# A fused four-layer image kernel: side stages begun earlier, one transfer for each part of a sum, and inverse deviations by logarithm and exponential

## The chip, the cores and the metric

The kernel runs on 1 core of one Trainium2 chip. The metric is the device time of one execution in microseconds. Before the change the median of three runs is 13,699.78 us (13,695.32 to 13,710.06). All engines of the core work: TensorE (PE) multiplies matrices, VectorE (DVE), ScalarE (ACT) and GpSimd (POOL) work on tiles of up to 128 partitions, and SyncE (SP) issues almost all transfers between the chip's memory (HBM) and the core's SBUF.

## What is computed

Four images of 96 channels and 64 x 64 points go through four layers, each `x = x + layer(group_norm(x))`. Layer 0 is an attention over a pooled image with a neighbourhood softmax, layer 2 a 3 x 3 convolution. Layers 1 and 3 each hold a four-way selective scan over the 4096 points: the image read by rows and by columns, forwards and backwards, with 192 channels of 16 states. Cut to the scan of layer 3 (layer 1 has the same recurrence in another form):

```
def step(h, inp):
    d, uu, bb, cc = inp
    h = h * jnp.exp(d[..., None] * A) + (d * uu)[..., None] * bb[:, :, None, :]
    y = jnp.einsum('bkdn,bkn->bkd', h, cc)
    return (h, y)
...
y = oy[:, 0] + inv[:, 0] + why + invwhy          # the sum of the four directions
y = layernorm_last(jnp.transpose(y, (0, 2, 1)).reshape(B, H, W, Di), ong, onb)
return y * jax.nn.silu(z) @ ow.T
```

Layer norms over channels follow the sum of the four directions in both layers, and another one stands in layer 3. They need 1 / sqrt(variance + 1e-5) for each point. Group norms (32 groups of 3 channels over all points) stand ahead of each layer.

## The kernel before, in words

**Units.** Layer and image give eight scans, in the order of `SCANS`: layer 1 of images 0 and 1, layer 3 of images 0 and 1, layer 1 of images 2 and 3, layer 3 of images 2 and 3. Here they are numbered 0 to 7. A scan has four directions, each cut into 4 chunks of 1024 points and 2 halves of 96 channels: 32 groups. A group is cut into 12 units of 8 channels times 16 states (128 partitions x 1024 points). So a scan has 384 units, and the kernel 3072. In the text "unit 361" is counted within a scan.

**A unit** (`unit`, L2167) issues, in an order written out by hand, the load of `rep` four units ahead (`fetch`, L2068), its decays two units ahead on ACT (L2076), its own scan on DVE (`scan`, L2096), the product with C on POOL (`times_c`, L2108), the product of the next unit's input with B on DVE (`times_b`, L2089), and the matmul that makes that input two units ahead (`drive`). Every four units `collect` sums states on PE into `acc`, and after a group's last collect `output` copies `acc` to `yo`, which a transfer stores into `y_row` or `y_col` at the start of the next unit. The list `stored` counts the groups that are stored. Each engine runs its instructions in the order in which they are issued; SP's queue holds all loads and stores.

**`prepare(g)`** makes a group's decays' exponents and inputs two groups ahead. For the first half of each chunk it needs the chunk's two halves of u (`load_u`, L1962). They are loaded ahead only within a scan; for the first chunk of the next scan `prepare` loads them itself, in unit 366 of the scan before, and its matmul stands one unit later.

**Stages.** Everything else is a generator that is resumed up to three times a unit through `Slots.begin`: a `yield` tells how many slots of 0.5 us of budget a step is put down at, a bare `yield` stands after matmuls, which are put down at their own estimate. `PACE[s]` is the budget of a unit of scan s. `beside(s)` says which stages run beside scan s: `first` (layer 0 and the input side of layer 1), `second` (the output side of layer 1, layer 2, the input side of layer 3), `third` (the output side of layer 3) and `last` (the same for the last image, in blocks). Scans 0, 3 and 4 have a `first` beside them; 1, 2, 5 and 6 a `second`, that of the image whose layer-1 scan has just ended; 7 has three `third` and the `last`. A stage begins at unit 0; at unit 365 `work.run()` issues all that is left of it at once. In the steps of the program, `second` stages are done at units 353 to 360 and leave nothing to `work.run()`; scans 0, 3 and 4 leave it 8, 24 and 8 steps.

**Sums of the four directions** (`directions`, L1529). Each half image has 4 parts (chunks) of 96 channels x 1024 points, stored as four blocks of 24 rows with gaps of 8. `ungapped` (L1118) loads a part with four transfers of 24 rows, 96 KB each. `directions` waits until the scan's last groups are stored, loads all parts of one half (32 transfers), goes on, and does the same for the other half. Then 16 steps add the two images on PE and copy them back on ACT.

**`layer_norm`** (L1261) collects the variances of 8 (or 2) pieces in one PSUM tile, makes `lines`, the inverse deviations of 8 x 512 (or 2 x 512) points, by a square root on ACT (L1292) and a reciprocal on DVE (L1294), and broadcasts each line to 96 partitions by a matmul. It is called 18 times beside or behind the scans. **`group_norm_on_scalar`** (L1161) does its passes over the image on ACT; 14 calls.

Of the kernel before, what the change touches and what calls it, by code (L numbers as in the profile page):

```python
# [9 lines left out]
F32 = mybir.dt.float32  # L10
# [17 lines left out]
CH = 1024  # L28
NCH = L // CH
# [9 lines left out]
          (("first", 3),), (("second", 2),), (("second", 3),), (("third", 0), ("third", 1), ("third", 2), ("last", 3)))  # L39
GN_EPS = 1e-5  # L40
PHI_EPS = 1e-12
PACE = (2.95,3.45,3.45,2.95,2.95,3.45,3.45,3.2)


PHI_SAFE = 10.0
# [855 lines left out]
def streams(ctx: ExitStack, tc: tile.TileContext, x, wts, cst, out, wat, cat, flag):  # L901
# [215 lines left out]

    def ungapped(dst, src, cols):  # L1118

        for q in range(4):  # L1120
            nc.sync.dma_start(out=dst[24 * q : 24 * q + 24], in_=src[32 * q : 32 * q + 24, cols])

    def group_norm(src, dst):

# [32 lines left out]
    def group_norm_on_scalar(src, dst):  # L1161

        st = small.tile([96, 8], F32, name="gs_st")
        for j in range(4):
            s = src[:, bass.ts(j, CH)]
            nc.scalar.activation(s, s, AF.Copy, accum_out=st[:, j : j + 1])
            yield 1
        mv = small.tile([96, 4], F32, name="gs_mv")
        nc.vector.tensor_reduce(mv[:, 0:1], st[:, 0:4], AX.X, ALU.add)
        yield 0.5  # L1170
        p = bank()
        mm(p[:96, 0:1], group[:96], mv[:, 0:1])
        yield
        nc.scalar.activation(mv[:, 1:2], p[:96, 0:1], AF.Copy, scale=-1.0 / L)
        yield 0.5
        for j in range(8):
            p = bank()
            nc.scalar.activation(p[:96], src[:, bass.ts(j, PCH)], AF.Square, bias=mv[:, 1:2], accum_out=st[:, j : j + 1])
            yield 1
        nc.vector.tensor_reduce(mv[:, 2:3], st, AX.X, ALU.add)  # L1180
        yield 0.5
        p = bank()
        mm(p[:96, 0:1], group[:96], mv[:, 2:3])
        yield
        nc.scalar.activation(mv[:, 2:3], p[:96, 0:1], AF.Sqrt, bias=eps[:96], scale=1.0 / L)
        yield 0.5
        nc.vector.reciprocal(mv[:, 2:3], mv[:, 2:3])
        nc.vector.tensor_mul(mv[:, 3:4], mv[:, 1:2], mv[:, 2:3])
        yield 0.5
        for j in range(4):  # L1190
            nc.scalar.activation(dst[:, 16 * j : 16 * j + 16, :], img(src)[:, 16 * j : 16 * j + 16, :], AF.Identity,
                                 scale=mv[:, 2:3], bias=mv[:, 3:4])
            yield 1

    def diagonals(pool, w, name="diag"):

# [64 lines left out]
    def layer_norm(pool, V, n, gains, each, chunks=range(8)):  # L1261

        chunks = list(chunks)
        m = len(chunks)
        acc = held()
        sq = {}

        def add(i):
            for h in range(n):
                mm(acc[:8], cv("means")[:96, n - 1, 7 - i : 15 - i], sq.pop((i, h)),  # L1270
                   i == 0 and h == 0, i == m - 1 and h == n - 1)

        for i, j in enumerate(chunks):
            js = bass.ts(j, PCH)
            p1 = bank()
            for h in range(n):
                mm(p1[:96], mean[n][:96], V[:, h, js], h == 0, h == n - 1)
            yield
            for h in range(n):
                nc.vector.tensor_sub(V[:, h, js], V[:, h, js], p1[:96])  # L1280
                t = pool.tile([96, PCH], F32, name="ln_sq", bufs=4)
                nc.scalar.activation(t, V[:, h, js], AF.Square)
                sq[i, h] = t
            yield n
            if i:
                add(i - 1)
                yield
                yield n
        add(m - 1)
        yield  # L1290
        r = lines[:8]
        nc.scalar.activation(r[:m], acc[:m], AF.Sqrt, bias=eps[:m])  # L1292
        yield n
        nc.vector.reciprocal(r[:m], r[:m])  # L1294
        yield 3
        for i, j in enumerate(chunks):
            js = bass.ts(j, PCH)
            p = bank()
            mm(p[:96], ident[:, i : i + 1].to_broadcast([128, 96]), lines)
            yield  # L1300
            for h in range(n):
                nc.vector.scalar_tensor_tensor(out=V[:, h, js], in0=V[:, h, js], scalar=gains[:, h : h + 1],
                                               in1=p[:96], op0=ALU.mult, op1=ALU.mult)
            yield 1
            yield from each(j)
# [223 lines left out]
    def directions(V, b, tag):  # L1529

        with Stack(1) as T:
            full = len(groups) // len(SCANS) * (SCANS.index((tag, b)) + 1)
            cols = []
            for h in range(2):
                while stored[0] < full - 1 + h:
                    yield WAIT
                t = T.tile([96, W, H], F32, name="yc", bufs=2)
                cols.append(t)
                for j in range(4):
                    ungapped(t.rearrange("p a b -> p (a b)")[:, bass.ts(j, CH)], y_col[h][b], bass.ts(j, CH))  # L1540
                    ungapped(V[:, h, bass.ts(j, CH)], y_row[h][b], bass.ts(j, CH))
                yield 4

            def turned(n):
                y = T.tile([96, PCH], F32, name="yt", bufs=2)
                nc.scalar.copy(img(y), cols[n // 8][:, :, 8 * (n % 8) : 8 * (n % 8) + 8].rearrange("p a b -> p b a"))  # L1546
                return y

            y = turned(0)
            for n in range(16):  # L1550
                v = V[:, n // 8, bass.ts(n % 8, PCH)]
                p = bank()
                mm(p[:96], ident[:96, :96], v, True, False)
                mm(p[:96], ident[:96, :96], y, False, True)
                yield
                nc.scalar.copy(v, p[:96])
                if n < 15:
                    y = turned(n + 1)
                yield 1

    def second(b):

# [589 lines left out]
    total = len(groups) * NG  # L2152
    per = total // len(SCANS)
    made, store, waiting, stored, owed = [], [], [], [0], 0.0

    def later(n, f):

# [9 lines left out]
    def unit(i, prep, work, budget):  # L2167


        if i + AHEAD < total:  # L2170
            fetch(i + AHEAD)
        while store:
            store.pop()()
            stored[0] += 1
        catch_up(1)
        j = i - BEHIND - 3
        due = j >= 0 and j % 4 == 0
        left = budget - DRIVE - (SUM if due else 0.0)
        if j > 0 and j % NG == 6:
            t = spent[0]  # L2180
            former(j)
            left -= spent[0] - t
        mine = 1 <= prep.slots <= 3
        left -= prep.begin(1.0) if mine else work.begin(left)
        if i + 2 < total:
            decays(i + 2)
        while made:
            store.append(output(made.pop()))
        scan(i)
        if i:  # L2190
            carry_on(i - 1)
        times_c(i)
        if i + 1 < total:
            times_b(i + 1)
        if mine:
            prep.end()
        work.end()
        left -= work.begin(left)
        if due:
            collect(j)  # L2200
        if i + 2 < total:
            drive(i + 2)
        work.end()
        left -= work.begin(left)
        if due and j % NG == NG - 4:
            made.append(j)
        work.end()
        if not mine:
            prep.begin(1.0)
            prep.end()  # L2210
        return left

    class Slots:
# [24 lines left out]
                next(self.stage, 0)  # L2238

        def run(self):  # L2240
            for _ in self.stage:
                pass

    idle = Slots(iter(()))

# [7 lines left out]
    with tc.manual_schedule():  # L2253
        for _ in prepare(0):
            catch_up(9)
        catch_up(9)
        prep = Slots(prepare(1))
        for _ in range(LEAD):
            prep.begin(0)
            prep.end()  # L2260
            catch_up(1)
        for i in range(AHEAD):
            fetch(i)
        decays(0)
        decays(1)
        drive(0)
        drive(1)
        times_b(0)
        for i in range(total):
            s, at = divmod(i, per)  # L2270
            g, m = divmod(i, NG)
            if at == 0:
                work, owed = Slots(beside(s)), 0.0
            if m == NG - LEAD and g + 2 < len(groups):
                prep.run()
                prep = Slots(prepare(g + 2))

            if at == per - NG - LEAD - 1 and s < len(SCANS) - 1:
                work.run()

            owed = min(owed, 0.6) + PACE[s]
            owed = unit(i, prep, work, owed)
        for j in range(total - 4, total, 4):
            collect(j)
            output(j)()
            stored[0] += 1
    solo[0] = True
    spare.clear()
    work.run()
# [49 lines left out]
```

## Time and profile before

| | us |
|---|---|
| median of three runs | 13,699.78 |
| the profiled execution | 13,707.96 |
| its span, first to last instruction | 13,706.2 |
| busy: DVE, PE, POOL | 11,460.3, 11,203.6, 10,278.9 |
| busy: ACT, weight loads | 8,833.5, 3,476.9 |
| DMA: mean share of 16 engines | 77.1% |
| first scan instruction begins | 645.8 |
| last scan instruction ends | 13,587.7 |

Busy time is counted for each engine by itself; the engines work side by side, so the columns don't add up to the span. The page's groups give, for each line, engine and operation, the busy time, the mean of one in ns, and the idle time of the engine just before it, with what ended that idle time. A window's row gives busy time and instruction counts of PE, weight loads, DVE, ACT and POOL, then the clock that TensorE was granted (1.00 is full), the share of time that the DMA engines were busy, and GB/s. In a timeline the columns are the start, the duration, engine, line, operation, tiles and count, and in brackets the idle time before, with what ended it. In the waits' view they are the total, the number of times and the longest. Nearly all matmuls are issued by one helper line (L1028); there the tile's name tells them apart: `bx` is the scan's input, `acc` the sum over states, `one` and `held` belong to stages and `prepare`.

### The profile page before, as it was taken

What the parts mean: (1) busy time and instruction counts of PE and PEld (TensorE: products, weight loads), DVE (VectorE), ACT (ScalarE), POOL (GpSimd) and SP (SyncE); (2) the same over time, 40 slices, a digit from 0 to 9 for tenths busy, and PEclk for the clock granted to TensorE, in tenths of its full rate; (3) what the DMA queues carried; (4) which work ended last, traced back from release to release, by engine and by line L of the source; (5) the groups of instructions that cost most, each with busy time, mean ns of one, the idle gap of its engine ahead of it and who ended that gap; (6) DMA issues with size and microseconds to landing.
All of it is one profiled execution on the core that took longest, in us unless ns stands there. A gap on an engine that the chain in (4) does not pass through costs nothing.

```text
span 13706.2 us, 129052 instructions
## 1 busy us (share of the span) xinstructions
PE 11203.6 (82%) x40767; PEld 3476.9 (25%) x41442; DVE 11460.3 (84%) x7351; ACT 8833.5 (64%) x12480; POOL 10278.9 (75%) x4730
## 2 busy tenths in 40 slices
PE   9878886988879887888878787798969888777766
PEld 3322221322223222222222222232313222111211
DVE  1488987998889888889978898898889988888886
ACT  3366576667756677665766657566765667666754
POOL 1178887888868878788868888788878878666674
PEclk9899998999889898999989999998989999888977
DMA  0278888787878878788878788787888878777774
GB/s 11 67 174 201 206 221 212 197 220 202 222 190 219 216 200 227 187 198 213 237 185 196 196 212 230 190 225 203 220 211 198 224 202 230 196 197 192 187 198 117
DMA packets 840855, 2682.60 MB, mean 196 GB/s; under 512 B 111264, under 2 KB 113792, under 8 KB 840160
## 3 DMA queue, kind: packets, MB, share of 16 engines
q1 hardware_dynamic: 839504, 2672.34, 77.1%
q8 instruction: 330, 5.41, 0.2%
q14 instruction: 365, 2.99, 0.1%
q10 hardware_dynamic: 656, 1.87, 0.0%
HBM read 2179.90 MB, written 493.88 MB: 195 GB/s over the span
## 4 chain that ended last, share of the span: by engine, by line
PE 30%; DVE 15%; ACT 14%; DMA 10%; POOL 6%; issue 6%; SPq 1%; DVEq 0%; POOLq 0%; ACTq 0%; another core or an unknown queue 0%
PE one L1028 21%; DVE hs L2096 9%; DMA rep<-dd 5%; PE acc L1028 5%; DVE bx L2089 4%; PE bx L1028 4%; ACT rep L2076 3%; POOL rep L2108 3%; ACT L2076 1%; ACT L2018 1%; DMA arena<-ycol 1%; DMA du<-cut 1%; ACT arena L1394 1%; PE held L1028 1%; DMA parts<-du 1%
## 5 line engine op out<-in xcount | busy, mean ns | idle before, releaser
L2108 POOL TENSOR_TENSOR rep<-hs,bc 128x1024 f32<-128x1024 f32 x3072 | 7219.4, 2357 | 2317.8 <-DVE hs L2096 1918.8
L1028 PE MATMUL one<-arena 128*96 128x512 f32 (+4 forms) x11072 | 5276.8, 602 | 640.1 <-ACT arena L1394 140.4
L2096 DVE TENSOR_TENSOR_SCAN hs<-rep,carry,bx 128x1024 f32<-128x1024 f32 x2304 | 5401.9, 2345 | 312.5 <-ACT carry L2104 31.8
L2089 DVE TENSOR_TENSOR bx<-bx,bc 128x1024 f32<-128x1024 f32 x3072 | 3719.9, 1211 | 816.8 <-PE bx L1028 547.8
L2076 ACT ACTIVATE rep<-rep,l_decay 128x1024 f32<-128x1024 f32 x3072 | 3501.1, 1144 | 975.5 <-DMA rep<-dd 962.0
L1028 PE MATMUL bx<-parts,spread 128*128 128x512 bf16 x5469 | 1828.1, 408 | 1054.9 <-DVE hs L2096 954.9
L1028 PEld LDWEIGHTS one<-arena 128*96 128x96 f32 (+3 forms) x11072 | 1787.4, 171 | 3062.7 <-issue 1763.9
L2096 DVE TENSOR_TENSOR_SCAN hs<-rep,bx 128x1024 f32<-128x1024 f32 x768 | 1754.8, 2285 | 156.9 <-ACT carry L2104 54.3
L1028 PE MATMUL acc<-rep,ct 128*32 128x512 f32 x12288 | 1702.5, 658 | 8.2 <-POOL rep L2108 5.5
L1028 PEld LDWEIGHTS <-spread 128*128 128x128 bf16 x6144 | 456.6, 99 | 3294.7 <-DVE hs L2096 1858.2
L1028 PE MATMUL one<-pr,ct 64*96 64x512 f32 x1024 | 618.9, 688 | 91.0 <-ACT pr L1983 33.5
L1394 ACT ACTIVATE arena<-one 128x512 f32<-128x512 f32 x576 | 342.5, 595 | 498.0 <-PE one L1028 497.3
L1028 PEld LDWEIGHTS acc<-rep,ct 128*32 128x32 f32 x12288 | 363.1, 116 | 1161.3 <-issue 970.0
L2076 ACT ACT_TABLE_LOAD x477 | 612.0, 1283 | 8.4
L1028 PE MATMUL one<-arena,ct 128*96 128x512 f32 x508 | 288.6, 676 | 272.6 <-ACT arena L1546 215.1
L1028 PE MATMUL bx<-arena 128*96 128x512 f32 (+5 forms) x1120 | 488.8, 575 | 22.1 <-ACT arena L1808 3.2
L1028 PE MATMUL held<-arena,cols 128*32 128x256 f32 x3072 | 482.1, 395 | 24.1 <-ACT arena L1394 23.0
L2104 ACT COPY carry<-hs 128x1 f32<-128x1 f32 x2304 | 410.4, 178 | 131.1 <-DVE hs L2096 129.9
L1028 PE MATMUL held<-arena 128*32 128x256 f32 x3072 | 482.6, 396 | 0.0
L1028 PE MATMUL one<-us,wt 128*38 128x512 f32 x1024 | 283.0, 676 | 103.5 <-DMA us<-urow 59.8
L982 POOL MEMSET arena<- 32x1024 f32 (+5 forms) x81 | 54.2, 690 | 396.6 <-ACT arena L1394 322.1
L2018 ACT ACT_TABLE_LOAD x256 | 328.4, 1283 | 4.4
(3325 smaller groups left out, 10269.3 us busy)
## 6 DMA issues: line engine op xcount, KB each, us to landing
rep<-dd SPq DMA_DIRECT2D x3072, 512.0 KB
parts<-du SPq DMA_DIRECT2D x1024, 144.0 KB
bc<-rows SPq DMA_DIRECT2D x256, 512.0 KB
dd<-delta SPq DMA_DIRECT2D x256, 384.0 KB
du<-cut SPq DMA_DIRECT2D x256, 384.0 KB
yrow<-yo SPq DMA_DIRECT2D x128, 512.0 KB
ycol<-yo SPq DMA_DIRECT2D x128, 512.0 KB
us<-urow SPq DMA_DIRECT2D x128, 384.0 KB
```

What stands on the lines that cost most here:

```text
L982: nc.gpsimd.memset(arena[96:, k : min(k + CH, a + n)], 0.0)
L1028: nc.tensor.matmul(o, lhsT=lhsT, rhs=rhs, start=first, stop=last)
L1394: nc.scalar.activation(last.rearrange("p a b -> p (a b)"), p, AF.Exp, scale=HD**-0.5)
L2018: nc.scalar.activation(w, w, AF.Ln)
L2076: nc.scalar.activation(a, a, AF.Exp, scale=decay[tag][:, k, NG * h + m : NG * h + m + 1])
L2089: nc.vector.tensor_mul(bx, bx, ready[i // NG][2][:, 0, :])
L2096: nc.vector.tensor_tensor_scan(out=hs, data0=a, data1=bx, initial=carry[:, h, m : m + 1] if c else 0.0, op0=ALU.mult, op1=ALU.add)
L2104: nc.scalar.copy(carry[:, h, m : m + 1], live[i][1][:, CH - 1 : CH])
L2108: nc.gpsimd.tensor_tensor(a, hs, ready[i // NG][2][:, 1, :], ALU.mult)
```

## The change

There are four edits.

1. *Begin of stages.* `work.run()` stands at unit 361 instead of 365, and right behind it the first u of the next scan is loaded (`load_u`), and the next scan's stage begins, 23 units sooner than at that scan's unit 0. `PACE` is raised: 2.95 becomes 3.0, 3.02 or 2.98, 3.45 becomes 3.6, 3.2 becomes 3.3; from unit 361 on that of the next scan counts.
2. *Loads of the sums.* `ungapped` issues one transfer of 4 x 24 rows. `directions` loads part by part: `fetched(h)` issues one part, or two for layer 3, and then gives the unit back; a part of the image whose store comes last is loaded once its store is four units old; the first use stands four units behind the last load (`pause`). The parts of the second half are loaded between the steps of the first half. While `work.run()` issues the rest of a stage, `rush` takes these waits in units away.
3. *Inverse deviations.* `lines` is made by two activations on ACT, a logarithm and an exponential with scale -0.5, and the broadcast follows two steps sooner.
4. *Group norm.* The passes of `group_norm_on_scalar` are put down at three, two and three slots instead of one.

```diff
-PACE = (2.95,3.45,3.45,2.95,2.95,3.45,3.45,3.2)
+PACE = (3.0,3.6,3.6,3.02,2.98,3.6,3.6,3.3)
...
     def ungapped(dst, src, cols):
-        for q in range(4):
-            nc.sync.dma_start(out=dst[24 * q : 24 * q + 24], in_=src[32 * q : 32 * q + 24, cols])
+        nc.sync.dma_start(out=dst,
+                          in_=src.rearrange("(q r) c -> q r c", q=4)[:, :24, cols])
...
     def group_norm_on_scalar(src, dst):
...
             nc.scalar.activation(s, s, AF.Copy, accum_out=st[:, j : j + 1])
-            yield 1
+            yield 3
...
             nc.scalar.activation(p[:96], src[:, bass.ts(j, PCH)], AF.Square, bias=mv[:, 1:2], accum_out=st[:, j : j + 1])
-            yield 1
+            yield 2
...
                                  scale=mv[:, 2:3], bias=mv[:, 3:4])
-            yield 1
+            yield 3
...
         r = lines[:8]
-        nc.scalar.activation(r[:m], acc[:m], AF.Sqrt, bias=eps[:m])
-        yield n
-        nc.vector.reciprocal(r[:m], r[:m])
-        yield 3
+        nc.scalar.activation(r[:m], acc[:m], AF.Ln, bias=eps[:m])
+        yield 1
+        nc.scalar.activation(r[:m], r[:m], AF.Exp, scale=-0.5)
+        yield 1
...
             full = len(groups) // len(SCANS) * (SCANS.index((tag, b)) + 1)
-            cols = []
-            for h in range(2):
-                while stored[0] < full - 1 + h:
+            cols = [T.tile([96, W, H], F32, name="yc", bufs=2) for _ in range(2)]
+
+            def fetched(h):
+                col = cols[h].rearrange("p a b -> p (a b)")
+                ways = [(y_row, V[:, h, :]), (y_col, col)]
+                if tag == "l3_":
+                    ways.reverse()
+                for n, (image_, to) in enumerate(ways):
+                    for c in range(NCH):
+                        while settled(full - 8 + 2 * c + h + 1 if n else full - 8):
+                            yield WAIT
+                        js = bass.ts(NCH - 1 - c, CH)
+                        ungapped(to[:, js], image_[h][b], js)
+                        if tag == "l1_" or c % 2:
+                            yield WAIT
+
+            def settled(n):
+                return stored[0] < n or (now[0] < landed[n - 1] + 4 and not rush[0])
+
+            def pause(n):
+                t = now[0]
+                while now[0] < t + n and not rush[0]:
                     yield WAIT
-                t = T.tile([96, W, H], F32, name="yc", bufs=2)
-                cols.append(t)
-                for j in range(4):
-                    ungapped(t.rearrange("p a b -> p (a b)")[:, bass.ts(j, CH)], y_col[h][b], bass.ts(j, CH))
-                    ungapped(V[:, h, bass.ts(j, CH)], y_row[h][b], bass.ts(j, CH))
-                yield 4
+
+            yield from fetched(0)
+            yield from pause(4)
+            more = fetched(1)
...
                 nc.scalar.copy(v, p[:96])
+                if n == 7:
+                    yield from more
+                    yield from pause(4)
                 if n < 15:
                     y = turned(n + 1)
                 yield 1
+                next(more, 0)
+                yield WAIT if tag == "l1_" else 2
...
         while store:
             store.pop()()
             stored[0] += 1
+            landed.append(i)
+        now[0] = i
...
         def run(self):
+            rush[0] = True
             for _ in self.stage:
                 pass
+            rush[0] = False
...
-            if at == 0:
-                work, owed = Slots(beside(s)), 0.0
+            if i == 0:
+                work, owed = Slots(beside(0)), 0.0
...
-            if at == per - NG - LEAD - 1 and s < len(SCANS) - 1:
+            if at == per - NG - LEAD - 5 and s < len(SCANS) - 1:
                 work.run()
-
-            owed = min(owed, 0.6) + PACE[s]
+                low[len(groups) // len(SCANS) * (s + 1)] = load_u(len(groups) // len(SCANS) * (s + 1))
+                work, owed = Slots(beside(s + 1)), 0.0
+
+            owed = min(owed, 0.6) + PACE[min(s + (at >= per - NG - LEAD - 5), len(SCANS) - 1)]
             owed = unit(i, prep, work, owed)
```

More of the change, by code (lines that the diff above doesn't have):

```diff
@@ L2154, in streams @@
     made, store, waiting, stored, owed = [], [], [], [0], 0.0
+    landed, now, rush = [], [0], [False]
     def later(n, f):
@@ L2286, in streams @@
             stored[0] += 1
+            landed.append(total)
     solo[0] = True
```

## The prediction

> **What bounds the kernel now.** I read the page first, then DVE's timeline cut at the scan instructions of line 2096, then SP's timeline where DVE stood still, then DVE's waits, last the packets. 3072 units run one after another; each needs one scan (L2096) and one product (L2089) on DVE:
>
> ```profile
> span 13706.2 us, 129052 instructions
> L2096 DVE TENSOR_TENSOR_SCAN hs<-rep,carry,bx 128x1024 f32<-128x1024 f32 x2304 | 5401.9, 2345 | 312.5 <-ACT carry L2104 31.8
> L2089 DVE TENSOR_TENSOR bx<-bx,bc 128x1024 f32<-128x1024 f32 x3072 | 3719.9, 1211 | 816.8 <-PE bx L1028 547.8
> q1 hardware_dynamic: 839504, 2672.34, 77.1%
> ```
>
> 2345 + 1211 = 3556 ns is the floor of a unit, 10,924 us for all. From the first scan (645.8 us) to the end of the last (13,587.7 us) pass 12,942 us; some 2,020 us lie above the floor. They sit in places. With 384 units a scan, the eight scans take 1595, 1584, 1584, 1573, 1581, 1567, 1580 and 1879 us, against a floor of 1365. Rows of the second scan (PE, PEld, DVE, ACT, POOL busy, clock, DMA share, GB/s), then DVE and SP at its start:
>
> ```profile
> 2240.40:2254.60 14.20, 7.29 (x24) 1.54 (x24) 13.65 (x9) 5.28 (x7) 13.01 (x7) 0.76 0.79 206
> 2254.60:2298.90 44.30, 20.51 (x58) 6.12 (x60) 17.35 (x10) 18.98 (x28) 19.62 (x9) 0.73 0.89 231
> 2298.90:2336.50 37.60, 29.85 (x95) 9.29 (x97) 25.71 (x17) 31.87 (x47) 24.01 (x11) 1.00 0.77 186
> 2447.60:2977.00 529.40, 509.35 (x1684) 172.85 (x1716) 487.44 (x283) 341.26 (x490) 464.04 (x209) 0.99 0.85 212
> 3750.50:3821.10 70.60, 46.81 (x137) 9.47 (x134) 62.80 (x36) 35.63 (x41) 59.02 (x27) 0.63 0.89 220
> ```
> ```profile
> 2266.44 1.23 DVE L2089 TENSOR_TENSOR bx<-bx,bc 128x1024 f32<-128x1024 f32 x1 [9.55 <-PE bx L1028]
> 2293.38 1.23 DVE L2089 TENSOR_TENSOR bx<-bx,bc 128x1024 f32<-128x1024 f32 x1 [13.89 <-PE bx L1028]
> ```
> ```profile
> 2236.59 3.32 SPq L1121 DMA_DIRECT2D arena<-ycol  x4
> ...
> 2254.08 1.51 SPq L1121 DMA_DIRECT2D arena<-yrow  x4
> 2255.88 1.81 SPq L2068 DMA_DIRECT2D rep<-dd  x3
> 2266.53 1.51 SPq L1121 DMA_DIRECT2D arena<-ycol  x4
> ```
>
> The first three rows are 16 units: 96.1 us, 39 above the floor. SP issues 32 quarter loads at 0.38 us, and no `rep` gets out meanwhile; then 32 more. The fourth row (140 units, 3.78 us each) is bound by PE: 96% busy. The fifth (18 units, no stage work) runs at 3.9 us with DMA already at 0.89.
>
> **The change, part by part** (where things stand in the order comes from the built program; time above the floor is meant throughout).
>
> *The sums' loads.* 64 quarter loads a place become 16 of 384 KB. Issue costs nothing: 16 at 0.54 us (the `rep` form) = 9 us over 17 or more units, against 64 x 0.38 = 24. What counts is the transfer. The trace holds the marks by which each transfer reports: on five of SP's eight semaphores their number comes out exactly if 96 or 128 rows give 16 marks, 24 rows 12 and one for the rest, 38 rows 2 and one. So 96 rows use 16 engines, 24 use 12, 38 use 2: the largest number up to 16 that divides the rows. The new load reads 4 x 24 x 1024 and writes 96 x 1024; no row shows such a pair. Its ends: 16 engines of 6 packets of 4 KB, or 4 engines of 24. A 38-row transfer goes by its odd shape, so I take 4.
>
> The Trainium skill (DMA: Bandwidth & Descriptors, "Why a DMA increments its semaphore by 16 and not by 1") says that the engines used are the largest number up to 16 that divides the slowest dimension of both patterns. By it this load has 4 engines, which speaks against the change; the rows above fit it, and by 16 engines the sum below would be some 170 us lower.
>
> A 4 KB packet lasts 159 ns at the median when alone, 190 to 199 ns on the mean with two or three others in flight, 255 with fifteen (packets of the trace). The scan's own traffic is 220 GB/s x 3.55 us = 0.78 MB a unit, 12 packets an engine. With a packet of p, four engines have 3.55 - 12p to spare in a unit, and a place asks 384p of them. A `rep` lands some 8 us before its scan, 7 before its decay must start; that much lateness is free, twice at the four `l1_` places (loads in two bursts over 34 units), once at the three `l3_` places (17 units). Copies add 8 and 4 us, as the units after the bursts do now. Now the places cost 39, 42, 41, 42 and 30, 32, 33 us.
> - p = 0.19: `l1_` 73 - 43 - 14 + 8 = 24, so -17 each, -68; `l3_` 73 - 22 - 7 + 4 = 48, so +16 each, +48. With the last image's 8 column loads (192 x 0.19 = 36 against 30 now) and its row loads, +10. Sum -10. I take this: four busy engines and the rest part of the time.
> - p = 0.159: `l1_` 61 - 56 - 14, nothing, + 8: -33 each; `l3_` 61 - 28 - 7 + 4 = 30: -2 each. Sum about -135. Sixteen engines: -180.
> - p = 0.255: `l1_` 98 - 17 - 14 + 8 = 75, +34 each; `l3_` 98 - 8 - 7 + 4 = 87, +55 each; last image +25. Sum +325.
>
> *The next scan's first load, and the rush.* Today `load_u` for a new scan stands one unit before its use, in unit 366, behind what `work.run()` left:
>
> ```profile
> 6890.32 12.54 SPq L1255 DMA_DIRECT2D urow<-arena  x3
> 6911.30 1.54 SPq L1962 DMA_DIRECT2D us<-urow  x2
> ```
> ```profile
> 6904.24 1.23 DVE L2089 TENSOR_TENSOR bx<-bx,bc 128x1024 f32<-128x1024 f32 x1 [13.91 <-PE acc L1028]
> 6926.16 1.23 DVE L2089 TENSOR_TENSOR bx<-bx,bc 128x1024 f32<-128x1024 f32 x1 [13.61 <-PE bx L1028]
> ```
>
> Units 361 to 370 of scans 0 to 6 lie 18, 4, 5, 29, 16, 5 and 7 us above the floor. After, the load is issued at 361 and used at 367 (21 us; `us` lands in 8), and only scan 0 still rushes, with 15 steps for 8. That leaves scan 0's 18 and about 1 each: -60. Ends: -45 and -70.
>
> *Logarithm for root and reciprocal.*
>
> ```profile
> 2386.64 3.34 DVE L1294 RECIPROCAL lines<-lines 8x512 f32<-8x512 f32 x1 [2.81 <-ACT lines L1292]
> ```
>
> 18 of these take 18 x 3.34 us, and DVE idles 31.8 us before them. ACT instead runs one more 0.68 us activation (the square root's row); another 1.28 us table load is none, since the decays' exponential needs it today. The Trainium skill (ScalarE: Activation LUTs, "Table sets: the hidden batching unit") lists a set with both functions; here L2018's logarithm and L2076's exponential each show a load, and one set would save 18 x 1.28 = 23 us of ACT, which waits anyway. The first broadcast now stands in the exponential's own unit: PE waits there, and behind it the next `bx` product, about 2 us for the 11 that idle today = 22. In the loop 16 x 3.34 + 26.3 - 22 = 58; in the tail root to broadcast shrinks from 3.34 to 1.28 + 0.68, twice 1.4. Together -60; ends -15 (PE takes it over) and -85.
>
> *Group norm spaced out.* Fourteen calls; DVE's waits on them are 69 us:
>
> ```profile
> DVE gs_mv L1169 <- ACT arena L1166: 28.0, 6, 8.6
> DVE gs_mv L1180 <- ACT one L1178: 21.0, 8, 4.5
> DVE gs_mv L1187 <- ACT gs_mv L1185: 19.9, 7, 13.3
> ```
>
> 13.3 of them belong to `prep.run()`, the 8.6 to the landing of x; neither goes away. -20, ends 0 and -45.
>
> *Earlier begin, higher pace.* Image sums still wait for the scan's last store, so in the four `second` stages the rest begins at unit 27 instead of 15 and ends at 351 instead of 353: 14 units fewer for the same work. In the fifth row PE spends 2.6 us a unit at clock 0.63, 1.6 at full clock; a unit offers a stage 3.55 - 1.6 = 2 us. 14 x 2 = 28 us move into other units, free where DVE bounds and paid where PE does: 194 of 339 units (the fourth row and the last 54). 16 each, +64; scans 3 and 4 get six units more, -9: +55. Ends 0 and +112. Scan 7's stage gains 23 units and is nowhere bound by PE: nothing.
>
> Sum: -10 - 60 - 60 - 20 + 55 = -95, less 10 for what scan 0's longer rush may add: -85. The profiled span 13,706.2 becomes 13,621. That run took 13,708.0, the median of three is 13,699.8, so I say **13,615 us**.
>
> **Rivals.**
> 1. *The loads are cheap* (sixteen engines, or packets at 159 ns because the scan waits meanwhile): -135 to -180 in place of -10, 13,700 - 210 to - 255 = 13,445 to 13,490. For it: the bytes are the same, and the bursts' SP queue is gone. Against: 24 and 38 rows never got 16 engines. Chance 0.2.
> 2. *Slower: four DMA engines become the bound.* DMA stands at 0.89 even without a stage, so packets stay near 255 ns; each place then stops the scan for 75 to 87 us, `rep` queued behind the loads on those engines. +325 in place of -10: 13,950 at worst. It decides from about 0.21 us a packet, where the loads cost 85 more than I take. For it: packets with eight in flight average 0.21. Against: while the scan waits it asks for nothing. Chance 0.25, mostly 13,730 to 13,850.
> 3. *The reciprocal does not pay and PE is bound throughout*: -15 for -60 and +112 for +55 give 13,715, no change. For it: PE waited 68.8 us for the reciprocal's rows, and waits for the exponential alike. Chance 0.1.
>
> **How the numbers follow.** Forecast 0.45: 13,615, its own range 13,500 to 13,672. The whole range, 13,450 to 13,810, leaves out the ends of rivals 1 and 2. A measurement here tells 0.2% (27 us) from none: faster (under 13,672) 0.45 + 0.2 = 0.65, same 0.1, slower 0.25.
>
> **What would show it.** After: no stretch with 32 L1121 issues; DVE idle at the `l1_` places about 24 us above the floor, at `l3_` about 48; units 361 to 370 at 3.6 us in scans 1 to 6; no reciprocal of `lines`, PE waiting 2 to 4 us at the broadcast instead. Places over 55 (`l1_`) or 65 us (`l3_`) show rival 2; under 15, rival 1. Wrong altogether: stage starts that leave the scan's last 23 units no longer near the floor for another reason than DMA, as PE or ACT.

## The result, and the profile after

The changed kernel is slower: 13,852.4 us median (13,849.2 to 13,870.7, 4 runs) against 13,701.1 us (13,695.3 to 13,710.1, 4 runs); ratio 1.0112, 95% interval 1.0100 to 1.0125, some 151 us. The forecast was 13,615 with a range to 13,810; the time lies beyond it, on the side of rival 2. Scans are numbered from 0; the `l1_` starts are those into scans 1, 2, 5 and 6, where the sums of layer 1 are loaded.

First the page of the changed kernel: its span, the two instructions that make a unit, and SP's queue with its share of 16 DMA engines.

```profile
span 13847.3 us, 128923 instructions
q1 hardware_dynamic: 833520, 2672.32, 75.9%
L2114 DVE TENSOR_TENSOR_SCAN hs<-rep,carry,bx 128x1024 f32<-128x1024 f32 x2304 | 5403.0, 2345 | 475.5 <-ACT rep L2094 172.7
L2107 DVE TENSOR_TENSOR bx<-bx,bc 128x1024 f32<-128x1024 f32 x3072 | 3724.2, 1212 | 719.0 <-PE bx L1028 708.8
```

The floor of a unit has not moved (2345 + 1212 ns). What moved is the idle time ahead of the scan: 475.5 us, 312.5 before, and the largest cause that this group names is now the decay on ACT, not the carry. Same bytes in q1, a little less packet time (75.9% of 13,847 against 77.1% of 13,706), and a longer span: the DMA engines did less per microsecond. The waits of DVE (line, what ended the wait, total us, times, longest) show it, before and after:

```profile
DVE hs L2096 <- ACT carry L2104: 86.1, 56, 9.5
DVE hs L2096 <- ACT rep L2076: 14.6, 11, 8.6
```
```profile
DVE hs L2114 <- ACT carry L2122: 203.4, 87, 20.2
DVE hs L2114 <- ACT rep L2094: 184.9, 43, 11.3
```

The two belong together: ACT runs in order, so a decay (L2094) that waits for its `rep` also holds the carry copy (L2122) queued behind it. From 101 to 388 us. The cause one step back is in ACT's and SP's timeline of the changed kernel inside the start of scan 2, while the column loads of the second half image run (start, duration, instruction, in brackets the idle time before it and what ended it):

```profile
3922.61 0.65 SPq L1120 DMA_DIRECT2D arena<-ycol  x1
3923.30 0.52 SPq L2086 DMA_DIRECT2D rep<-dd  x1
3923.86 0.65 SPq L1120 DMA_DIRECT2D arena<-ycol  x1
3927.42 7.52 SPq L2086 DMA_DIRECT2D rep<-dd  x4
```
```profile
3929.63 1.15 ACT L2094 ACTIVATE rep<-rep,l_decay 128x1024 f32<-128x1024 f32 x1 [9.97 <-DMA rep<-dd]
3930.68 0.17 ACT L2122 COPY carry<-hs 128x1 f32<-128x1 f32 x1
...
3942.35 1.15 ACT L2094 ACTIVATE rep<-rep,l_decay 128x1024 f32<-128x1024 f32 x1 [5.17 <-DMA rep<-dd]
3943.41 0.17 ACT L2122 COPY carry<-hs 128x1 f32<-128x1 f32 x1
```

SP is no longer stuffed: a load takes 0.65 us of its queue and a `rep` gets out between two of them. The `rep` is late all the same, by 10 and 5 us, because of what happens to it after its issue.

Each transfer reports by completion marks, one for each DMA engine that it used, and one more when fewer than 16 did. Their number comes out exactly on all eight semaphores of SP if a load of 4 x 24 rows in one transfer has 4 engines and one of 24 rows has 12:

```
issue to landing, us (p10 / median / p90)    engines   column loads           row loads
before, a load of 24 rows                    12        3.2 / 3.9 / 7.8        1.9 / 3.7 / 4.6
after, a load of 4 x 24 rows                 4         12.4 / 18.7 / 22.9     6.1 / 18.2 / 24.6
```

The pages agree: the marks are packets too, and q1 has 5,984 packets less than before at the same bytes, which is 136 loads times 44 (four times 12 marks against 4).

`rep` has its old median, 8.8 us; its longest went from 16.3 to 27.6. In the timelines above, the `rep` issued at 3923.30, between two loads, lands 19.0 us later at 3942.33, and its decay starts at 3942.35; that of the decay at 3929.63 took 14.0 us.

Time above the floor (3.55 us a unit, between the scan instructions of DVE's timeline), in the stretches that changed:

```
                                             before   after
four l1_ starts (units 361 to 26)               270     255
start of scan 7 (361 to 26)                      55      94
scan 7, units 27 to 360                         438     492
second stages, units 27 to 360, four scans      614     720
```

### The profile page after: what moved, and what is told of

Same layout as the page of the kernel before. It is cut to its first block, busy times and chain, and to the rows that moved or that the text cites. A ratio compares the mean times of both kernels' runs of the same rounds, so it can differ in the third digit from the quotient of the medians.

```text
span 13847.3 us, 128923 instructions
## 1 busy us (share of the span) xinstructions
PE 11281.4 (81%) x41442; PEld 3477.3 (25%) x41442; DVE 11429.1 (83%) x7333; ACT 8864.7 (64%) x12512; POOL 10287.1 (74%) x4730
## 3 DMA queue, kind: packets, MB, share of 16 engines
q1 hardware_dynamic: 833520, 2672.32, 75.9%
## 4 chain that ended last, share of the span: by engine, by line
PE 40%; DVE 17%; ACT 16%; DMA 14%; POOL 6%; issue 5%; SPq 1%; DVEq 0%; POOLq 0%; ACTq 0%
PE one L1028 25%; DVE hs L2114 11%; PE bx L1028 8%; DMA rep<-dd 7%; PE acc L1028 5%; DVE bx L2107 5%; ACT rep L2094 4%; POOL rep L2126 3%; PE held L1028 2%; DMA parts<-du 1%; ACT L2094 1%; DMA du<-cut 1%; ACT arena L1390 1%; DMA arena<-ycol 1%; ACT L2036 1%
## 5 line engine op out<-in xcount | busy, mean ns | idle before, releaser
L2114 DVE TENSOR_TENSOR_SCAN hs<-rep,carry,bx 128x1024 f32<-128x1024 f32 x2304 | 5403.0, 2345 | 475.5 <-ACT rep L2094 172.7
L2094 ACT ACTIVATE rep<-rep,l_decay 128x1024 f32<-128x1024 f32 x3072 | 3501.9, 1144 | 1275.6 <-DMA rep<-dd 1265.7
L2107 DVE TENSOR_TENSOR bx<-bx,bc 128x1024 f32<-128x1024 f32 x3072 | 3724.2, 1212 | 719.0 <-PE bx L1028 708.8
L1028 PE MATMUL bx<-parts,spread 128*128 128x512 bf16 x6144 | 1998.3, 410 | 1311.2 <-DVE hs L2114 1123.7
L2094 ACT ACT_TABLE_LOAD x475 | 609.4, 1283 | 8.4
L2122 ACT COPY carry<-hs 128x1 f32<-128x1 f32 x2304 | 410.5, 178 | 170.6 <-DVE hs L2114 170.3
L2036 ACT ACT_TABLE_LOAD x256 | 328.4, 1283 | 4.4
```

Of the source, the lines that this page charges most:

```text
L1028: nc.tensor.matmul(o, lhsT=lhsT, rhs=rhs, start=first, stop=last)
L2036: nc.scalar.activation(w, w, AF.Ln)
L2094: nc.scalar.activation(a, a, AF.Exp, scale=decay[tag][:, k, NG * h + m : NG * h + m + 1])
L2107: nc.vector.tensor_mul(bx, bx, ready[i // NG][2][:, 0, :])
L2114: nc.vector.tensor_tensor_scan(out=hs, data0=a, data1=bx, initial=carry[:, h, m : m + 1] if c else 0.0, op0=ALU.mult, op1=ALU.add)
L2122: nc.scalar.copy(carry[:, h, m : m + 1], live[i][1][:, CH - 1 : CH])
```

## The experiments

All times are medians; each ratio is to the kernel before on the same chip, with its 95% interval.

**Undo the one transfer** (`a_quarters`):

```
-        nc.sync.dma_start(out=dst, in_=src.rearrange("(q r) c -> q r c", q=4)[:, :24, cols])
+        for q in range(4):
+            nc.sync.dma_start(out=dst[24 * q : 24 * q + 24], in_=src[32 * q : 32 * q + 24, cols])
```

> The changed kernel, with the image sums' loads as four transfers of 24 rows again in place of one of 4 x 24 (their times in the order, one part after the other, stay as changed). Theory 1, the one transfer runs on four DMA engines and holds up what is queued behind it there: the loads land in 4 to 6 us as before in place of 18 to 19 us, the seven scan starts fall from 49 to 94 us above the floor (453 in all) to 15 to 35 each, the stretch of scan 7 with the last image's loads from 124 to about 75; time falls by 200 to 330 us, to 13,520 to 13,650. Theory 2, the loads' engines matter little and the loss is the convolutions of the second stages, bound by TensorE at the higher pace (+27 us each): falls by less than 60, over 13,790, and units 47 to 188 of scans 1, 2, 5, 6 stay at 54 to 56 us above the floor either way.

13,636.2 us, ratio 0.9943 (0.9926 to 0.9960): 216 us below the changed kernel and 73 below the kernel before. The four `l1_` starts fall from 255 to 120 us; units 47 to 188 of the second stages stay at 54 to 57 us, as both theories said. Not as said: only the starts into scans 2, 5 and 6 lie within 15 to 35 us (28, 25 and 22); the other four are at 44 to 58. This one part of the diff costs more than the whole result.

**The one transfer in the kernel before** (`b_onepiece`, the reverse edit on the kernel before).

> The kernel before with the sums' loads as one transfer of 4 x 24 rows each and nothing else: 8 of them in a burst, twice at each scan start. Theory 1 (four DMA engines): a burst takes 8 x 24 packets of some 0.2 us on each of four engines, 38 us in place of about 20, so each burst costs 15 to 20 us more; seven starts with two bursts +210 to +280, the last image +30 to +60: 13,930 to 14,040. The other theory, the bytes are the same and only the number of transfers counts: the queue of 32 issues is gone, -5 us or more a burst, 13,600 to 13,700.

13,945.0 us, ratio 1.0170 (1.0153 to 1.0187): +236, theory 1. Units 0 to 26 of scans 1, 2, 5, 6 rise from 54 to 56 us to 87 each.

**The engines or the size of the transfer?** The same single transfer from other rows (`a_rows96`), and two transfers of two row groups (`a_halves`):

```
+        nc.sync.dma_start(out=dst, in_=src[:96, cols])
```
```
+        for q in range(2):
+            nc.sync.dma_start(out=dst[48 * q : 48 * q + 48],
+                              in_=src.rearrange("(q r) c -> q r c", q=4)[2 * q : 2 * q + 2, :24, cols])
```

> The changed kernel with each sums' load reading rows 0 to 95 of its image in place of 4 x 24 of the 128 (so the sums get other rows, and the output is not the reference's; everything after works as it did). The load is still one transfer of the same 96 x 4 KB at the same place; only the first dimension of its source is 96 and no longer 4. Theory 1 (number of DMA engines): it runs on 16, lands in 3 to 6 us in place of 18 to 19, and the time is that of the quarter loads or below: 13,600 to 13,640. Rival (one large transfer holds up what stands behind it, whatever its engines): 13,800 to 13,870.

> The changed kernel with each sums' load as two transfers of 2 x 24 rows. Theory 1 (number of DMA engines): each gets two engines with 24 packets of 4 KB a row block, 48 in all on each engine if the two transfers meet on the same pair; a load lands in 19 to 35 us and the time rises above the changed kernel's, to 13,880 to 14,200. Rival (the number of transfers counts, four are fast and one is slow): between the two, 13,700 to 13,800.

13,571.8 us, ratio 0.9899 (0.9884 to 0.9914), and 14,331.6 us, ratio 1.0448 (1.0432 to 1.0464). Both rivals fall: the one large transfer is the fastest of all as soon as its first dimension is 96, and cutting it in two makes it far slower when that leaves 2. The sizes were missed on both sides. `a_rows96` is 28 us below the range expected (SP issues 16 loads a start, not 64, and each engine has 6 packets a load, not 8), though its loads land in 11 us at the median and not in 3 to 6; `a_halves` is 131 us above its range. The marks give 16 and 2 engines, and q1's packets again differ by the marks alone: 12 more for each of 136 loads on 16 engines than on 4, and as many for two transfers on 2 as for one on 4.

```profile
q1 hardware_dynamic: 835152, 2672.32, 78.2%
q1 hardware_dynamic: 833520, 2672.32, 73.4%
```

The waits of DVE's scan in the two:

```profile
DVE hs L2113 <- ACT carry L2121: 91.9, 76, 8.4
...
DVE hs L2113 <- ACT rep L2093: 53.1, 24, 9.8
```
```profile
DVE hs L2115 <- ACT carry L2123: 415.6, 95, 35.4
DVE hs L2115 <- ACT rep L2095: 363.3, 46, 19.4
```

145, 388 (after) and 779 us. The windows of one start, units 361 to 383 of scan 1 and 0 to 26 of scan 2, for 16, 4 and 2 engines (columns: window, us, busy time of PE, PEld, DVE, ACT, POOL, clock, DMA share, GB/s):

```profile
3709.50:3801.00 91.50, 49.65 (x159) 10.79 (x152) 80.24 (x47) 44.93 (x48) 75.61 (x34) 0.71 1.01 250
3801.00:3906.70 105.70, 74.27 (x252) 19.32 (x251) 92.70 (x54) 83.31 (x118) 87.80 (x39) 0.88 0.94 228
```
```profile
3753.70:3866.80 113.10, 50.46 (x158) 11.02 (x151) 80.30 (x46) 45.04 (x48) 76.98 (x34) 0.65 0.81 210
3866.80:3989.10 122.30, 78.49 (x253) 20.60 (x252) 92.83 (x55) 82.76 (x118) 86.64 (x38) 0.82 0.73 190
```
```profile
3810.20:3954.00 143.80, 53.34 (x158) 11.32 (x151) 80.26 (x47) 46.07 (x50) 76.89 (x34) 0.60 0.64 166
3954.00:4103.80 149.80, 80.99 (x253) 21.27 (x252) 92.90 (x55) 83.30 (x118) 86.65 (x38) 0.76 0.58 154
```

The instructions are the same, DVE is busy for the same 80 and 93 us, and the mean DMA share goes *down* as the stretch gets longer. The reading that fits is that a few engines are full while the rest wait for the scan to go on. The trace doesn't tell the engines apart, so how full the few are is inferred; what points to them is the falling share beside a growing wait on `rep`.

**The sums as before** (`a_oldsums`: the changed kernel with the old `directions` and quarter loads, all else as changed).

> The changed kernel with the image sums as in the kernel before (loads of four transfers of 24 rows in a burst, first step when the scan's last store is issued); the earlier begin, higher pace, logarithm, group norm and early first load stay. It splits the forecast in two: the prediction's terms without the loads (-60 first load, -60 logarithm, -20 group norm, +55 pace, -10) say 13,615; then the one-transfer loads alone would have cost 240 against the old bursts. The logarithm alone gave +6 in place of -60 and the pace +25 a scan where +16 was said, so from these runs I expect some 13,700 to 13,720: then the loads' term, -10 on record, was +140.

13,717.3 us, ratio 1.0004 (0.9995 to 1.0013). (The text above gives the prediction's last 10 the wrong sign: -60 - 60 - 20 + 55 + 10 = -75 says 13,625.) So the change splits: the loads' edit +135, everything else together +13, not resolved from nothing. `a_quarters` against this run says that the loads' new timing alone is worth 81 us.

**The old pace** (`a_pace`).

> The changed kernel with the old pace of each scan (2.95, 3.45, 3.45, 2.95, 2.95, 3.45, 3.45, 3.2). Theory 2, the higher pace packs the convolutions into units that TensorE bounds: units 47 to 188 of scans 1, 2, 5, 6 fall from 54 to 56 us above the floor to some 28 each, -108, of which up to half comes back as work that is pushed into later units or a rush before the next scan; time 13,745 to 13,800. Theory 1, it is the loads: time within 30 us of 13,852, starts of the scans unchanged at 49 to 94 us.

13,851.1 us, ratio 1.0102 (1.0085 to 1.0119): no change against the changed kernel. Units 47 to 188 of the second stages did fall, from 54 to 56 us to 30 to 32, and the ends of those scans (361 to 383) rose by 35 to 37. So theory 1 has the time right, but its starts do not stay as they were (60 to 130 us, where 49 to 94 was said): all that the stages gain comes back there, not half of it. Units 47 to 188 of scan 1 and its end, changed kernel and this one:

```profile
2496.20:3052.70 556.50, 523.78 (x1736) 176.96 (x1734) 496.77 (x295) 351.94 (x496) 469.32 (x211) 0.96 0.83 208
3753.70:3866.80 113.10, 50.46 (x158) 11.02 (x151) 80.30 (x46) 45.04 (x48) 76.98 (x34) 0.65 0.81 210
```
```profile
2498.90:3029.60 530.70, 513.19 (x1721) 174.39 (x1721) 493.20 (x289) 340.47 (x479) 466.39 (x210) 0.99 0.86 215
3712.80:3860.50 147.70, 78.76 (x228) 21.38 (x227) 80.33 (x47) 55.54 (x60) 76.93 (x34) 0.70 0.68 178
```

At the old pace PE does 70 more matmuls in the row of the end: the stage isn't done at unit 361 and the rest is rushed through. The pace says where PE's work is paid, not whether.

**The logarithm alone, and the logarithm with distance** (`b_log` on the kernel before; `a_quarters_loglate` on the changed kernel with quarter loads).

```
         nc.scalar.activation(r[:m], r[:m], AF.Exp, scale=-0.5)
-        yield 1
+        yield WAIT
+        yield WAIT
```

> The kernel before with ScalarE's logarithm and exponential in place of root and VectorE's reciprocal, nothing else. As predicted: 16 reciprocals of 3.34 us and 26 of the 32 us waited before them go, 22 us come back at the broadcasts: -60, 13,640. Rival: TensorE, which waits for the row either way, keeps the end of those units, and shorter stages only close up the same work: 13,685 or more.

> The changed kernel with quarter loads, and two units of distance between the exponential and the first broadcast of the layer norm (18 places). Theory A, the logarithm gave nothing because the broadcast stands in the exponential's unit and TensorE, then VectorE's product, wait for ScalarE there (VectorE's wait at the product after the broadcast grew from 46 to 104 us): the 80 us waited at that product shrink below 30, time -40 to -60, to 13,575 to 13,600. Theory B, the time of those units belongs to TensorE's and ScalarE's own work and moves on: 13,620 to 13,650, the waits at other lines grow by as much.

(`yield WAIT` ends the stage's steps for the unit.) `b_log` took 13,714.7 us, ratio 1.0003 (0.9993 to 1.0012): nothing, where -60 was said; the rival's 13,685 or more holds. The first broadcast in the timeline of `b_log`:

```profile
2389.82 1.28 ACT L1294 ACT_TABLE_LOAD   x1
2391.12 0.63 ACT L1294 ACTIVATE lines<-lines 8x512 f32<-8x512 f32 x1
...
2391.80 2.02 PE L1028 MATMUL one<-lines,ct 128*96 128x512 f32 x2 [5.23 <-ACT lines L1294]
...
2393.86 1.40 DVE L1302 SCALAR_TENSOR_TENSOR arena<-arena,wt,one 96x512 f32<-96x512 f32 x2 [3.23 <-PE one L1028]
```

DVE no longer computes a reciprocal for 3.34 us; it stands for 3.23 us at the product that needs the result. Over the kernel this wait of L1302 on PE grew from 45.8 us to 103.8, before and in `b_log`:

```profile
DVE arena L1302 <- PE one L1028: 34.1, 21, 4.0
DVE arena L1302 <- PE bx L1028: 11.7, 3, 7.4
```
```profile
DVE arena L1302 <- PE one L1028: 82.7, 36, 5.3
DVE arena L1302 <- PE bx L1028: 21.1, 4, 7.4
```

With two units of distance it is 74.8 (103.6 without), and the time 13,612.7 us, ratio 0.9926 (0.9912 to 0.9940), 23 us below `a_quarters`; the intervals of the two overlap. Between the two theories: 29 us of wait went, about that much time with it (23, not clear of noise), and the wait did not fall below 30.

**Group norm's spacing, the early first load, the earlier begin, each undone** in the changed kernel with quarter loads (`a_quarters_gn`: `yield 1` for 3, 2 and 3; `a_quarters_lateu`: without the `load_u` at unit 361; `a_quarters_at0`: stages begun at unit 0).

> The changed kernel with quarter loads and the group norm's old spacing (a step's cost 1 in place of 3, 2 and 3). The prediction gave the spacing -20 (0 to -45): undone, 13,636 rises to about 13,656. Rival: it only lengthens the stages, which then rush at their scan's end: undone, it falls by up to 20.

> The changed kernel with quarter loads and without the early first load of the next scan, which then stands one unit before its use, in unit 366, as in the kernel before; nothing else changes. If the gain at the scans' ends comes from this load: +10 to +14 at each of up to seven ends, 13,700 to 13,730. If it comes from the shorter rush and the loads' spacing: 13,636 within 15.

> The changed kernel with quarter loads and each stage begun at its scan's first unit again, with that scan's pace; the rush stays at unit 361. Theory: the 23 units are capacity for the stages (2 us each, 46 us a scan) and the place where the sums' row loads start; undone, the work is packed tighter or rushed: +60 to +130, 13,700 to 13,770. Rival: the stages have room, and the units near the scan's end return to the floor as fast as others leave it: 13,620 to 13,660.

13,686.4 us (0.9983, 0.9974 to 0.9992), 13,633.0 (0.9946, 0.9932 to 0.9959) and 13,628.0 (0.9944, 0.9930 to 0.9958), beside 13,636.2. The spacing is worth 50 us; DVE's waits at `gs_mv` are 51 us with it, 80 without, and units 188 to 239 of the second stages 22 and 44 us above the floor on the mean. The early load and the earlier begin are worth nothing that can be seen, as the second reading of each expectation said. Without the early load units 361 to 370 of scans 0, 1, 4 and 5 cost 5 to 11 us more each, but the stretch to 383 costs the same to within 5: the stall only comes later.

**One part a unit for the second layer's sums too** (`best_l3`, on `a_quarters_loglate`).

> The changed kernel with quarter loads, the logarithm's two units of distance, and the second layer's sums' loads one part a unit as the first layer's. If the places of these loads (18 to 30 us above the floor each in scan 6's end and scan 7) come from two parts in one unit: -20 to -40 against 13,613; if scan 7 lacks the 32 units this takes, the tail grows and it is 13,613 or more.

13,633.5 us, ratio 0.9939 (0.9926 to 0.9953): no gain. The start of scan 7 falls from 61 to 39 us, the tail after the last scan grows from 115 to 135. So `a_quarters_loglate`, 0.9926, stays ahead of both kernels. A load of the right rows on 16 engines (images kept as 96 rows) was not tried: it needs other stores or other tiles.

## Why the prediction failed

The runs split the miss of 237 us (13,852 against 13,615) in two: the loads +135 for -10, and the rest +13 for -75.

**The sums' loads: right engines, no capacity to spare.** That the load gets four engines was the prediction's own reading, and the runs with 2, 4, 12 and 16 engines settle it; they agree with the rule of the Trainium skill that was cited there (DMA: Bandwidth & Descriptors, "Why a DMA increments its semaphore by 16 and not by 1"), which spoke against the change. The step that failed is the term "four engines have 3.55 - 12p to spare in a unit", with p = 0.19 for the scan's packets and the load's alike: nothing was to spare. The four `l1_` starts against the packets that the busiest engine gets for one start:

```
kernel        engines   packets   four starts, us   one start
a_rows96      16             96          99            25
a_quarters    12            128         120            30
after          4            384         255            64
a_halves       2            768         479           120
```

(The 768 assume that both transfers of a load meet on the same two engines. On two different pairs the busiest engine would have the 384 packets of the changed kernel; `a_halves` takes 479 us more than it.) From 96 to 384 packets a start costs 39 us more, 0.136 us a packet; from 384 to 768 56 more, 0.146. Each packet is paid from the 96th on, at less than the 0.19 us of the sum, but without the 43 us of spare capacity and the 14 of free lateness that the sum took off: a start costs 64 us, and 25 with 16 engines, where the sum had 24 for the four. The row of `a_rows96` fits this: with the loads spread over all engines the DMA share is 1.01 there. I argued that a waiting scan asks for nothing and so left 0.19; rival 2's "DMA stands at 0.89 even without a stage" was the better reading, and its range, mostly 13,730 to 13,850, just misses the time. Its sign, over 55 us at the `l1_` places and over 65 at the `l3_` places, decides less. The `l1_` starts are at 55 to 83, but by the same units, 361 to 26, the kernel before has 61 to 73; its 39 to 42 in the prediction are for 16 units. The `l3_` places do not reach 65. Against sixteen engines the four cost 280 us (13,852 - 13,572); the prediction's sum had 170.

The three `l3_` places (23 units from unit 361 of scan 6 and from units 83 and 191 of scan 7) stand at 18 to 26 us with 16 engines, 55 to 63 with 4 and 113 to 121 with 2. The 48 of the sum is near the 55 to 63, but by luck: the packet was taken too dear (0.19, against 0.13 here from 16 engines to 4) and 29 us of capacity and lateness were taken off that were not there. So the +135 against `a_oldsums` lies elsewhere:

```
                                          said           a_oldsums   after
four l1_ starts                           -68            253         255
scan 7 to unit 360, with its start        +48 and +10    531         586
second stages, units 27 to 360            (in the pace)  650         720
```

The last row is as large as the first one's miss, and engines have no part in it: the second stages stand at 720 to 734 us with the new sums on 2, 4, 12 or 16 engines. The new sums issue their last loads in unit 12 (7 before, 6 in `a_oldsums`) and end later, and the rest of the stage is closer packed. The prediction had this ("begins at unit 27 instead of 15") as part of its +64 in the pace; over units 27 to 360 the four scans pay 106 (614 to 720), 36 of them with the old sums already. Sixteen engines were to give -180 against the old bursts; `a_rows96` against `a_oldsums` gives -145.

**Logarithm, -60: in fact +6.** The removed work was sized rightly, 18 reciprocals and the wait ahead of them. What came back was not: "about 2 us for the 11 that idle today" made 22 us; 58 came back at L1302 alone, and the prediction counted no wait of DVE behind PE's there. Some 30 more stand at two other instructions: DVE's idle time ahead of its product with B rose from 816.8 to 835.3 us, and its wait on PE at L1280, an earlier step of the layer norm, from 46.8 to 58.4. Each figure is from one profiled execution, so that the logarithm caused these 30 is not shown. Nor was the new table load free because "the decays' exponential needs it today": the kernel's table loads rose from 1,001 to 1,015, and those of the decays fell only from 477 to 475.

**First load and rush, -60: right in part of its places, not in the sum.** With the old sums, units 361 to 370 of scans 0 to 5 fell from 79 to 32 us, but those of scan 6, where the next stage's loads now lie, rose from 6 to 30: -24 in all. (Of the seven figures in the prediction scan 1's 4 should be 6.) And the first steps of the next stage lie there and in the units after: undoing the load or the begin moves nothing.

**Group norm, -20: about -50** with quarter loads, a little outside the ends given (0 and -45). The waits named were sized rightly, 29 us of them went. But in units 188 to 239 of the second stages the spacing saves 87 us over the four scans, of which 59 are left at unit 360; the `l1_` starts give back 25 of them (120 us with it, 95 without).

**Pace, +55.** With the old sums the convolutions (units 47 to 188) paid 15 to 18 us a scan; that this is near the 16 that was said is luck, since the 16 stood for the later begin, which the old sums don't have. With the new sums they paid 26 to 28. But PE's work is paid once: at the old pace the ends of the scans take it all back, so that the higher pace costs nothing.

The single edits don't add up: group norm -50, the others near nothing, all of them together with the old sums +13. Which pair works against each other stays open.

## What to carry to other kernels

Before several transfers are merged into one, count the engines: here 4 x 24 rows in one transfer ran on 4 of them, four transfers of 24 rows on 12, and the merged one cost 216 us although it saved three quarters of the issues. When a transfer runs on few engines, ask what else is queued on those and price it with the share that the stretch has when all engines carry it; at a share near 1 each packet of the busiest engine was paid here, with about 0.14 us. And when an operation moves from one engine to another, look at the first instruction that needs its result: if that stands in the same unit, the engine that was freed may wait there for as long as it worked before, as here (3.23 us for 3.34).

## What the hardware showed that was not expected

The mean DMA share fell from 1.01 to 0.81 and 0.64 as the same loads took longer. A low share beside late transfers can mean few busy engines as well as too little to do.

ScalarE's exponential of `lines` loaded a table again in 14 of 18 cases in `b_log` (13 of 18 in the changed kernel), 1,283 ns each: in all those in which a logarithm came just before it on ACT. In the others a decay stood between the two and had loaded already. Where that happens, the step from logarithm to result takes 1.28 + 0.63 us, where 0.63 would do and the reciprocal took 3.34. Why it loads although the prediction names a set with both functions, no run shows. The two rows of `b_log`:

```profile
L1294 ACT ACT_TABLE_LOAD x14 | 18.0, 1283 | 0.3
L1294 ACT ACTIVATE lines<-lines 8x512 f32<-8x512 f32 x10 | 6.3, 627 | 0.1
```

Stores of a rush can hold SP for long: in `a_pace` three stores of `urow` behind the unfinished stage took 14.82 us of its queue, and no `rep` left in that time.

```profile
3719.14 14.82 SPq L1251 DMA_DIRECT2D urow<-arena  x3
```
